# The first stage's stores, issued over three chunks instead of four and ahead of the x loads

## The chip, the cores and the metric

One core of a Trainium2 chip runs the kernel. The metric is the device time of one launch in microseconds (us), the median of several runs; smaller is better. Beside the times there is one execution taken by the hardware profiler, which gives start and length of every instruction on five engines: TensorE (PE; its weight loads are PEld), VectorE (DVE), ScalarE (ACT), GpSimd (POOL) and SyncE (SP). In this kernel SP and POOL also issue nearly all the DMAs: each puts them into a queue of its own, in the order of its program, and both queues are worked off by the same 16 DMA engines.

## The reference

Two layers run on x of shape (16, 192, 64, 64) in float32: 16 images, 192 channels, 64 by 64 pixels. Cut to what matters:

```python
h = layernorm_over_channels(x)                    # per pixel
pg = einsum('bchw,oc->bohw', h, in_proj_w) + b    # 192 -> 384 channels
projected, gate = split(pg, 2, axis=1)
projected = depthwise3x3(projected, dw_k)
scanned = four_directional_scans(projected)       # along rows and columns, both ways
local = depthwise3x3(projected, le_k)
mixed = (scanned + local) * sigmoid(gate)
x = x + conv1x1(gelu(batchnorm(mixed)), out_proj)
x = x + mlp(layernorm_over_channels(x))           # 192 -> 768 -> 192
# second layer: a depthwise masked 3x3 whose taps come from the mean of each image
```

The change touches only the part that computes `pg`, the normalised and projected x.

## The kernel before

The kernel has three stages. The first computes `pg` for all images and writes it to DRAM in an order that suits the second. The second takes groups of 8 channels at a time through the depthwise convolutions, the scans and the gate, and writes `mixed`. The third does the output projection, the MLP and the second layer.

The order of instructions on every engine is the order in which the program writes them: a `manual_schedule` covers PE, DVE, ACT, SP and POOL. A DMA instruction waits on its issuing engine until its buffers may be used, and what is written behind it on that engine waits too.

**The first stage** (lines 275 to 640) works on 64 chunks, `n` from 0 to 63. A chunk holds 4 groups of 128 pixels in each of two images. Four chunks (`per`) make a block; `blk, part = divmod(n, per)` gives the block and which quarter of it the chunk is. In one pass of the loop over n (L614):

- `load_a(n + 3)` (L499 to L507) loads the x of the chunk three ahead, in six DMAs of 128 KB (L505): three on SP for the first image, three on POOL for the second. Each moves runs of 512 bytes. The tile `xa` has four buffers, so that this load waits until PE has finished with chunk n - 1.
- `store_first` (L562 to L566) and `store(blk - 1, d, ...)` (L577 to L581) write the results of the block before. `PARTS` (L47) cuts the 24 groups of channels into five parts, d = 0 to 4, with 1, 7, 7, 5 and 3 groups; the very first group is kept on the chip by `store_first`. A store of one part is four DMAs, two on SP and two on POOL, of 64 KB per group: 64, 448, 448, 320 and 192 KB each.
- `turn(n + 1)` (L512) transposes the next chunk on PE (24 short matmuls, L518), from which DVE takes mean and variance over channels.
- `project(n, ...)` (L534) does the 48 matmuls of the chunk (L547) into PSUM, 12 for each group of pixels. DVE (L552, first image) and ACT (L553, second image) scale each group by its standard deviation and write it into the staging buffer of the block. There are two PSUM tiles per image, so PE can be two groups ahead of DVE and ACT.
- Work for later (weights, tables of decays, the matrices `dm` and `lm` of the second stage) is hung on given chunks by `beside(n, ...)` and run at the end of the chunk (L633).

**The staging buffer** is one of two: even blocks use `stg`, which exists once, odd blocks use `mid` (L538 to L541). The first write of block b therefore waits until all stores of block b - 2 have landed. Those stores are issued while block b - 1 is computed.

In the loop before the change, the loads and stores stand in this order:

```python
            if n + 3 < n_ac:
                load_a(n + 3)
            blk, part = divmod(n, per)
            if blk:
                if part == 0:
                    store_first(blk - 1)
                    store(blk - 1, 0, (nc.gpsimd, nc.sync))
                store(blk - 1, part + 1, (nc.gpsimd, nc.sync))
```

The names used further on: L44 is line 44, but "the load of pass 45" is `load_a(48)`, issued in pass n = 45 of the loop, and "S2" is `store(blk - 1, 2, ...)`.

Of the kernel before, what the change touches and what calls it, by code (L numbers as in the profile page):

```python
# [55 lines left out]
def conv_block_kernel(ctx: ExitStack, tc: tile.TileContext, x, prm, w_in, w_out, w_fc1, b_fc1, w_fc2, w1, bn1, w2, out):  # L56
    nc = tc.nc
# [217 lines left out]
    with ExitStack() as stage:  # L275
# [216 lines left out]
        n_ac = n_pairs * NCH  # L492
        per = BR // AR
# [5 lines left out]
        def load_a(n):  # L499
            blk, part = divmod(n, per)  # L500
            p, u = divmod(blk, 2)
            xa = xp.tile([128, 3, CH], F32, tag="xa", name="xa")
            for i, q in enumerate(HALF):
                for t in range(3):
                    (nc.sync, nc.gpsimd)[i].dma_start(  # L505
                        xa[q, t].rearrange("p (g n) -> p g n", n=128), xr[2 * p + i, u, :, t, part * AR:(part + 1) * AR])
            ast[n]["xa"] = xa  # L507
# [4 lines left out]
        def turn(n):  # L512

            xt = [psa.tile([128, 4, AR, 64], F32, tag=f"xt{i}", name=f"ps_xt{i}") for i in range(2)]
            for t in range(3):
                for g in range(AR):
                    for i, q in enumerate(HALF):
                        nc.tensor.transpose(xt[i][:, t, g], pixels(n, t, g)[q], ident[q, q])  # L518
            ast[n].update(xt=xt, st6=sp.tile([128, AR, 2, 6], F32, tag="st6", name="st6"),
                          mv=sp.tile([128, AR, 2, 2], F32, tag="mva", name="mva"))  # L520
# [7 lines left out]
        def deviation(n):  # L528
            rs = sp.tile([128, AR, 2], F32, tag="rsa", name="rsa")
            nc.scalar.activation(rs, ast[n]["mv"][:, :, :, 1], AF.Sqrt, bias=eps6)  # L530
            nc.vector.reciprocal(rs, rs)
            ast[n]["rs"] = rs

        def project(n, groups, beside_it):  # L534

            blk, part = divmod(n, per)
            if blk not in stag:
                if blk % 2:  # L538
                    both_i = mid.rearrange("p (i o j) -> p i o j", i=2, j=BR)
                else:  # L540
                    both_i = stg.tile([128, 2, 2 * C, BR], F32, tag="stg", name="stg")  # L541
                stag[blk] = [both_i[:, i] for i in range(2)]
            for g in groups:
                ps = [psa.tile([128, CH], F32, tag=f"pj{i}", name=f"ps_pj{i}", bufs=2)[:, 0:2 * C] for i in range(2)]
                for t in range(3):
                    for i, q in enumerate(HALF):
                        nc.tensor.matmul(ps[i], pixels(n, t, g)[q], wi[q, t].rearrange("p g k c -> p (g k c)"),  # L547
                                         start=(t == 0), stop=(t == 2))
                for v in beside_it(g) if n + 1 < n_ac else ():
                    variance(n + 1, v)  # L550
                j, rs = part * AR + g, ast[n]["rs"]
                nc.vector.tensor_scalar_mul(stag[blk][0][:, :, j], ps[0], rs[:, g, 0:1])  # L552
                nc.scalar.activation(stag[blk][1][:, :, j], ps[1], AF.Copy, scale=rs[:, g, 1:2])  # L553

        def each(blk):
            p, u = divmod(blk, 2)
            for i in range(2):
                ih, i8 = divmod(2 * p + i, n_half)
                for par, q in enumerate(HALF):
                    yield i, par, q, i8, 2 * u + par, HALF[ih]  # L560

        def store_first(blk):  # L562

            for i, par, q, i8, b, qh in each(blk):
                (nc.gpsimd, nc.sync)[par].dma_start(pg_even[qh, i8 * NB + b].rearrange("p k c j -> p (k c j)"),
                                                    stag[blk][i][q, 0:2 * GC].rearrange("p o j -> p (o j)"))  # L566
# [10 lines left out]
        def store(blk, d, queues):  # L577
            lo_, hi_ = PARTS[d]
            for i, par, q, i8, b, qh in each(blk):
                queues[par].dma_start(pg_d[d][i8, b, qh],  # L580
                                      stag[blk][i][q, lo_ * 2 * GC:hi_ * 2 * GC].rearrange("p o j -> p (o j)"))  # L581
# [30 lines left out]
        deviation(0)  # L612

        for n in range(n_ac):  # L614
            if n + 3 < n_ac:
                load_a(n + 3)
            blk, part = divmod(n, per)
            if blk:
                if part == 0:
                    store_first(blk - 1)  # L620
                    store(blk - 1, 0, (nc.gpsimd, nc.sync))
                store(blk - 1, part + 1, (nc.gpsimd, nc.sync))
                if part == per - 1:
                    stag.pop(blk - 1)

            h = AR // 2 if n == 0 else 0
            project(n, range(h), lambda g: ())
            if n + 1 < n_ac:
                turn(n + 1)
            project(n, range(h, AR), lambda g: (g,) if h == 0 else (2 * (g - h), 2 * (g - h) + 1))  # L630
            if n + 1 < n_ac:
                deviation(n + 1)
            for f, args in side.pop(n, ()):  # L633
                f(*args)
# [828 lines left out]
```

## Time and profile before

| | |
|---|---|
| median of three runs | 3542.76 us (3542.14 to 3543.65) |
| profiled execution, its own time | 3541.4 us |
| its span, first to last instruction | 3539.6 us |
| PE busy in the span | 3512.9 us (99%) |
| DVE, ACT, POOL busy | 2741.6, 1839.7, 1171.1 us |
| first stage | from 0 to about 581 us of the span |
| DMA in the first 600 us | 157.11 MB, mean 262 GB/s |

Times in the lines of the profile are in us from the start of the span. In a timeline, "x3" says that three like instructions stand side by side, and the two numbers ahead are the start of the first and the length of the whole run. In a list of waits, the name ahead of the arrow waited for the name behind it: total, number of times, longest. The chain of work that ended last is followed back from the end of the kernel; a stretch on it, if shortened, would have let the kernel end sooner. In a table of stretches, each engine has its busy time and its number of instructions; PEclk is the TensorE clock that was granted, as a share of full speed, and DMA is the mean busy share of the 16 DMA engines. Busy time of PE counts its matmuls with modelled ends.

### The profile page before, as it was taken

The numbers are of one execution on the slowest core, as the hardware profiler recorded it, in microseconds if no ns is written. First come the engines' busy times: TensorE is split into PE (matmuls) and PEld (weight loads), VectorE is DVE, ScalarE is ACT, GpSimd is POOL, SyncE is SP. The second block draws the span as 40 slices with busy tenths as digits, with TensorE's granted clock in tenths as the row PEclk, the third lists the DMA queues.
The fourth block names the chain that finished last, engine by engine and source line by source line (L and its number), as shares of the span: only waits on it lengthen the run. The fifth ranks groups of instructions, "written<-read, shape, count | busy, mean of one in ns | idle before, by whom it ended". The sixth has DMA issues, their size and how long they took to land.

```text
span 3539.6 us, 78530 instructions
## 1 busy us (share of the span) xinstructions
PE 3512.9 (99%) x33144; PEld 1919.0 (54%) x33144; DVE 2741.6 (77%) x4666; ACT 1839.7 (52%) x2086; POOL 1171.1 (33%) x1302
## 2 busy tenths in 40 slices
PE   9999999999999999999999999999999999999998
PEld 7666966566666754444444444444444444444444
DVE  7888777999999975557777777777677777767766
ACT  4444445888888844344444445454444444453543
POOL 3545432111111134333333334343333333343433
PEclk9999999999999999999999999999999999999999
DMA  6999999999999941112222223222222222232213
GB/s 178 269 271 276 272 272 310 288 289 285 277 285 286 248 119 34 40 55 61 70 68 74 66 65 82 59 75 63 79 61 70 68 74 65 66 83 58 75 34 90
DMA packets 288745, 492.00 MB, mean 139 GB/s; under 512 B 24752, under 2 KB 182824, under 8 KB 288392
## 3 DMA queue, kind: packets, MB, share of 16 engines
q1 hardware_dynamic: 246548, 341.57, 35.6%
q0 software_dynamic: 40912, 144.37, 14.2%
q8 instruction: 261, 4.28, 0.5%
q10 hardware_dynamic: 932, 1.03, 0.1%
q14 instruction: 92, 0.75, 0.1%
HBM read 284.95 MB, written 197.92 MB: 136 GB/s over the span
## 4 chain that ended last, share of the span: by engine, by line
PE 98%; DMA 1%; DVE 1%; issue 0%; ACT 0%; POOL 0%; SPq 0%; ACTq 0%; DVEq 0%
PE ps_f L1046 28%; PE ps_f L901 19%; PE ps_pj L547 14%; PE ps_l L718 12%; PE ps_d L674 7%; PE ps_s L901 7%; PE ps_o L956 5%; PE ps_o L949 2%; PE ps_xt L518 1%; PE ps_m L985 1%; PE ps_v L985 1%; DMA xa<-in_x_dram 0%; DVE ol L65 0%; PE ps_i L1259 0%; DVE o L65 0%
## 5 line engine op out<-in xcount | busy, mean ns | idle before, releaser
L1046 PE MATMUL ps_f<-h,wf 64*64 64x512 f32 x9216 | 1014.9, 590 | 0.0
L1048 ACT ACTIVATE gl<-ps_f,bf 128x1024 f32<-128x1024 f32 x384 | 428.2, 1115 | 1077.0 <-PE ps_f L1046 1076.7
L1046 PEld LDWEIGHTS ps_f<-h,wf 64*64 64x64 f32 x9216 | 346.2, 133 | 599.0 <-issue 574.9
L901 PE MATMUL ps_f<-gl,place 128*64 128x256 f32 (+1 forms) x3072 | 528.3, 486 | 1.1 <-ACT rs L1028 1.1
L547 PE MATMUL ps_pj<-wi,xa 64*128 64x384 f32 x3072 | 516.9, 487 | 7.1 <-DVE stg L552 6.8
L547 PEld LDWEIGHTS ps_pj<-wi,xa 64*128 64x128 f32 x3072 | 337.0, 188 | 151.6 <-DVE stg L552 9.3
L1081 POOL TENSOR_TENSOR gl<-gl 128x512 f32<-128x512 f32 x192 | 308.7, 1634 | 159.4 <-PE ps_f L901 159.4
L901 PEld LDWEIGHTS ps_f<-gl,place 128*64 128x64 f32 x3072 | 220.4, 137 | 222.4 <-issue 147.4
L1071 POOL COPY turn<-o 128x1 f32<-128x1 f32 x84 | 16.6, 197 | 820.9 <-DVE o L65 820.9
L1077 POOL TENSOR_TENSOR t<-gl 128x512 f32<-128x512 f32 x192 | 246.3, 1283 | 90.8 <-ACT gl L1048 46.4
L1079 POOL TENSOR_TENSOR t<-gl,t 128x512 f32<-128x512 f32 x192 | 247.5, 1289 | 43.8 <-ACT gl L1048 30.5
L65 DVE SCALAR_TENSOR_TENSOR o<-ximg,taps,o 128x1024 f32<-128x1024 f32 x180 | 231.7, 1288 | 4.9
L709 DVE TENSOR_TENSOR_SCAN v<-tab,q 128x1024 f32<-128x1024 f32 x96 | 218.3, 2274 | 5.6 <-ACT q L689 5.6
L711 DVE TENSOR_TENSOR_SCAN v<-tab,q 128x1024 f32<-128x1024 f32 x96 | 217.5, 2266 | 0.0
L505 POOL DMA_DIRECT2D xa<-in_x_dram x192 | 120.7, 635 | 274.4 <-PE ps_pj L547 238.7
L697 ACT ACTIVATE tab<-mask,dec_b 128x1024 f32<-128x1024 f32 x192 | 210.2, 1150 | 0.0
L1104 DVE SCALAR_TENSOR_TENSOR ximg<-ps_f,pt,ximg 128x256 f32<-128x256 f32 (+1 forms) x176 | 96.7, 549 | 145.6 <-PE ps_f L901 145.6
L553 ACT ACTIVATE stg<-ps_pj,rsa 128x384 f32<-128x384 f32 x128 | 119.5, 938 | 162.3 <-PE ps_pj L547 142.9
L553 ACT ACTIVATE mid<-ps_pj,rsa 128x384 f32<-128x384 f32 x128 | 119.2, 933 | 153.7 <-PE ps_pj L547 143.0
L962 DVE SCALAR_TENSOR_TENSOR ximg<-ps_o,pt,low 128x256 f32<-128x256 f32 x264 | 113.0, 479 | 93.8 <-PE ps_o L956 90.0
L956 PE MATMUL ps_o<-low,wo 128*64 128x256 f32 x1536 | 180.8, 384 | 0.0
L525 DVE BATCH_NORM_STATS2 st<-ps_xt 128x6 f32<-128x192 f32 x512 | 171.5, 335 | 4.6 <-PE ps_xt L518 4.0
(273 smaller groups left out, 5672.5 us busy)
## 6 DMA issues: line engine op xcount, KB each, us to landing
low<-in_x_dram SPq DMA_DIRECT2D x128, 384.0 KB
out_dram<-o SPq DMA_DIRECT2D x172, 256.0 KB
mid<-pg_d SPq DMA_DIRECT2D x8, 4096.0 KB
low<-mixed_d SPq DMA_DIRECT2D x116, 256.0 KB
low<-pg_d SPq DMA_DIRECT2D x7, 4096.0 KB
pg_o<-pg_d SPq DMA_DIRECT2D x7, 4096.0 KB
xa<-in_x_dram POOLq DMA_DIRECT2D x192, 128.0 KB, 5.1
xa<-in_x_dram SPq DMA_DIRECT2D x192, 128.0 KB
```

Of the source, the lines that this page charges most:

```text
L65: nc.vector.scalar_tensor_tensor(o, in0, scalar, in1, ALU.mult, ALU.add, **kw)
L547: nc.tensor.matmul(ps[i], pixels(n, t, g)[q], wi[q, t].rearrange("p g k c -> p (g k c)"), start=(t == 0), stop=(t == 2))
L553: nc.scalar.activation(stag[blk][1][:, :, j], ps[1], AF.Copy, scale=rs[:, g, 1:2])
L674: nc.tensor.matmul(dst(ps[o, ih]), mats[g % 2]["dm"][q, di + 1, :, ch], src(s["pg"][q, :, 0, ch]), start=(di == 0), stop=stop)
L718: nc.tensor.matmul(dst(bst[k]["ps"][o, i]), lm_of(g)[q, m, :, c], src(q, ih), start=start, stop=stop)
L901: nc.tensor.matmul(ps[q], w(i), rhs(i), start=start, stop=stop, **kw)
L956: nc.tensor.matmul(ps[wh][q].rearrange("p (r w) -> p r w", w=32), wo[:, 64 * t:64 * t + 64], cols(rows(s["mx"][:, i]))[:, :, wh], start=fi ...
L1046: nc.tensor.matmul(pf[o, i], wf1[q, t, m0:m0 + 64], s["h"][q, t], start=(t == 0), stop=(t == 2))
L1048: nc.scalar.activation(gl, pf, AF.Gelu, bias=bf1[:, m:m + 1])
L1077: sub(t1[:, m], b12(m), b11(m))
L1079: sub(t2[:, m], b22(m), t1[:, m])
L1081: sub(b12(m), b22(m), b12(m))
```

## The change

In the first quarter of a block nothing moves. In the second, S2 is issued ahead of the loads of x rather than behind them. In the third, S3 and S4 are issued ahead of the loads; before, S3 was issued behind them, and S4 behind those of the fourth quarter. In the fourth quarter only the loads are left.

```diff
         for n in range(n_ac):
-            if n + 3 < n_ac:
+            blk, part = divmod(n, per)
+            if part == 0 and n + 3 < n_ac:
                 load_a(n + 3)
-            blk, part = divmod(n, per)
             if blk:
                 if part == 0:
                     store_first(blk - 1)
-                    store(blk - 1, 0, (nc.gpsimd, nc.sync))
-                store(blk - 1, part + 1, (nc.gpsimd, nc.sync))
+                for d in ((0, 1), (2,), (3, 4), ())[part]:
+                    store(blk - 1, d, (nc.gpsimd, nc.sync))
                 if part == per - 1:
                     stag.pop(blk - 1)
+            if part and n + 3 < n_ac:
+                load_a(n + 3)
```

Nothing else differs: the same instructions with the same sizes are issued, and on PE, DVE and ACT the order is the same. `stag.pop` only forgets a name while the program is built.

## The prediction

> **What bounds the kernel now.** I read the page first.
>
> ```profile
> PE 3512.9 (99%) x33144; PEld 1919.0 (54%) x33144; DVE 2741.6 (77%) x4666; ACT 1839.7 (52%) x2086; POOL 1171.1 (33%) x1302
> ```
>
> PE is busy for 99% of the span, so a reordering of DMAs can win only where PE stands still in the first stage, and lose only by making it stand still. From the chain, taken in order of time, I read when each chunk's projection starts. The undisturbed pace is (429.82 - 344.46) / 10 = 8.536 us a chunk: 7.79 of projection, 0.74 of transposes. Two places with the same cause stand out, the first chunks of blocks 8 and 12 (n = 32, 48). The larger, in the chain between 425 and 460 us:
>
> ```profile
> 429.82 7.81 PE ps_pj L547 x47
> ...
> 441.87 4.73 DMA pg_d<-mid
> 446.60 0.01 issue
> 446.61 0.93 DVE stg L552
> 447.54 0.04 issue
> 447.58 5.83 PE ps_pj L547 x24
> 453.41 0.74 PE ps_xt L518 x24
> 454.15 5.85 PE ps_pj L547 x35
> ```
>
> From chunk 47 to chunk 49 it takes 454.15 - 429.82 = 24.33 us instead of 17.07, a loss of 7.26. DVE and ACT may not write `stg` until the stores of block 10 are out of it; the chain names `mid`, but `mid` is not what DVE writes here, so I take the name as an inference and look at SP's own timeline, from 405 us:
>
> ```profile
> 421.75 3.24 SPq L505 DMA_DIRECT2D xa<-in_x_dram  x3
> 425.03 2.54 SPq L580 DMA_DIRECT2D pg_d<-stg  x2
> 427.75 4.50 SPq L505 DMA_DIRECT2D xa<-in_x_dram  x3
> 432.30 2.17 SPq L580 DMA_DIRECT2D pg_d<-stg  x2
> 434.51 1.84 SPq L218 DMA_DIRECT2D dm<-dv_d  x1
> 436.53 2.27 SPq L505 DMA_DIRECT2D xa<-in_x_dram  x3
> 438.84 1.25 SPq L580 DMA_DIRECT2D pg_d<-stg  x2
> ```
>
> These are the loads of pass 45, S2, the loads of pass 46, S3, a matrix for the second stage, the loads of pass 47 and S4. S4 leaves only from 438.84 on, when PE is already in pass 48 (since 437.6): SP is most of a chunk late, and the store lands near 446.6. The small parameter loads just ahead (415.57 to 421.58) had held SP. The granted clock adds to it:
>
> ```profile
> 442.00:447.00 5.00, 0.28 (x2) 0.00 (x0) 0.40 (x1) 0.41 (x1) 0.92 (x2) 1.00 1.07 364
> ...
> 449.00:450.00 1.00, 1.00 (x6) 0.69 (x4) 0.93 (x5) 0.00 (x0) 0.00 (x0) 0.50 0.72 185
> ```
>
> PE is idle for 5.30 us (its wait for DVE) and then runs at 0.50 of its clock until about 451: 24 matmuls take 5.83 us instead of 3.9. So 5.30 + 1.93 = 7.2 of the 7.26. At n = 32 (chain: 290.84 to 309.72, 18.88 for two chunks) the loss is 1.81, with 1.52 idle and the clock at 1.00.
>
> [...] POOL stood 238.7 us in 49 waits of L505 for PE, with later stores behind it. [...] Of the first 600 us the DMA view gives SP's queue 73204 packets for 80.47 MB (1.10 KB each), POOL's 20766 for 75.42 MB (3.63 KB each)[...]. [...]
>
> **The change, part by part.** It issues the same 128 KB loads and the same stores. It does more than move S4 one pass up. `load_a` waits for PE to leave chunk n - 1, and that wait no longer stands ahead of S2, nor of S3 and S4. So S2 follows S1 at once in the first quarter, and S3 and S4 follow the second quarter's loads. Bytes by quarter, with a chunk's loads as 0.79 MB and a group as 0.26: before 3.1, 2.6, 2.1, 1.6; after 5.0, 2.9, 0.8, 0.8. At the 276 to 298 GB/s seen with full DMA engines, a chunk of 8.54 us passes some 2.4. A queue now builds up in the first half of a block and is drained in the second.
>
> *Gain, stores.* In block 11 I replay SP's rows in the new order, each with its own length: S2 421.75 to 424.3, loads of pass 45 to 427.5, S3 to 429.7, S4 to 431.0, loads of pass 46 to 434.2 (its 4.50 us contain waiting for PE; I leave 3.2). S4 leaves at 431.0 instead of 440.1. With the 6.5 us that it took before (440.09 to 446.6) it lands at 437.5; DVE wants the buffer after 439.8. The wait goes, with its half-speed clock: 7.26. At n = 32 S4 ends at 299.8 and the write comes at 303.85; some 5 us earlier (the fourth quarter's loads, 5.25, no longer stand ahead of it) removes 1.81. Together 9.07; both ends are sure within about 1 us, if nothing else holds the buffer.
>
> *Cost, SP's loads of x.* The loads of the second quarter move behind S2, those of the third behind S3 and S4. What counts is how much time is left between the end of their issue on SP and the transposes that need them, two chunks on. Before, from SP's timeline and the chain: pass 45, 425.0 to 428.96, 4.0 left; pass 46, 432.25 to 437.6, 5.4; pass 41, 6.7; pass 42, 7.8; the rest 8 to 15. PE waited for none, so one such load landed within 4.0 us of its issue. Taking off the issue time of the stores now ahead leaves: pass 45, 4.0 - 2.5 = 1.5; pass 46, 437.6 - 434.2 = 3.4, more if PE has lost time at pass 45's; pass 30, 298.5 - 287.1 - 4.95 - 2.24 = 4.2; pass 42, 4.9; pass 41, 5.4; the other second and third quarters 5.7 and more. The landing time is not shown for SP; on POOL a load takes 2.9 to 11.3 us, median 5.1. Lower bound 2.9: cost 1.4, at pass 45's loads alone. At 4.0: 2.5. At 5: pass 45 3.5, pass 30 0.8, pass 42 0.1, together 4.4. I take about 4.6: 3.1 and 0.4, together 3.5. Such a wait has no cover: the transposes stand ahead of the projection on PE, and DVE's statistics and the whole chunk follow. [...]
>
> *POOL's issues.* Four more stores at 0.53 to 0.55 us each are 1.1 to 2.2 us ahead of POOL's loads, hidden in its waits of 3.5 to 5.6 us for PE. POOL's ninth DMA in flight waits for the first (2.21 us at 442 us), so the denser order will show more such waits. Its loads have 17.1 us from pass to need; the slowest now needs about 11 plus the wait of pass 30. I charge nothing; without the cover it is about 1 us a block, 14 in all.
>
> *The end of the stage.* In block 15 no loads are left from pass 61 on; S4 moves ahead of the two loads of `wf1` (L70, L71), which are wanted at 594.2 and issued by 573. Nothing.
>
> Sum: -7.26 - 1.81 + 3.5 = -5.6 us. Against the profiled execution 3541.4 - 5.6 = 3535.8; the median of the runs is 1.4 above it, so 3542.76 - 5.6 = **3537.2**.
>
> **The rivals.**
> *All of the gain.* SP's loads land in time (below 3 us from issue, or S2 runs faster when it stands right behind the small loads). For it: SP idles between quarters in most blocks. Against it: pass 45 has 1.5 us left. -9.07 + 1.4 or less: 3533.7 to 3535.
> *SP's loads of x late in every block* (the one on the other side). Place: transposes of chunks 48, 33, 45 first, then all second and third quarters. Price by block at a landing time of 7.5 us: 0.9, 1.7, 0.4, 3.3, 1.8, 0.7, 2.6, 6.0 plus 1.9 of half clock, 1.5, 1.8, together 22.6; net +13.5, so 3556. It decides from 5.9 us of landing time on, where the loads cost the 9.1 gained. For it: POOL's median of 5.1 and the deeper queue ahead of the loads. Against it: the 4.0 bound, though that queue held small loads.
> *The wait stays.* DVE's wait was named after `mid`; if a DMA of the current block holds `stg`[...], S4's earlier issue saves little: 3541 to 3544. Against it: S4's times fit.
> That the change doesn't do what it says I exclude: the built order has the stores where the diff puts them, on SP and POOL alike.
>
> **How the numbers follow.** Chances: forecast 0.45 (3535.7 to 3540.5), all of the gain 0.23, the wait stays 0.14, loads late 0.18. About 0.2% (7.1 us) is what a measurement can tell from no change. Faster by more: all of the gain, and a little of the forecast, 0.26. Slower by more: most of the late case, 0.16. Within: 0.58. Range 3533 to 3549: it holds the first three cases and the mild part of the fourth, and leaves out about 0.17.
>
> **What would show it.** Right: no wait of DVE or ACT at L552 and L553 for a DMA at n = 32 and 48, no 0.50 clock near 450; S4 issued by SP about 9 us before pass 48; PE waits at L518 for `xa`, of 1 to 4 us at chunk 48. Wrong: PE waits for `xa` in most blocks (my landing time is too short), or the wait at n = 48 is still there (another holder of `stg`). The second and third stages should keep their lengths, 3539.6 - 581 us.

## The result, and the profile after

The changed kernel takes 3584.93 us in the median of four runs (3583.45 to 3593.89), the kernel before in the same series 3542.45 (3539.88 to 3543.65): a ratio of 1.0129, 95% interval 1.0117 to 1.0141, or 42.5 us slower. The forecast was 3537.2 with a range up to 3549. What happened is the rival "SP's loads of x late in every block", and at three times the size that it was given. One run of an experiment below (POOL alone ahead) took 3910.57 us at a granted clock of 0.887, the others of that kernel 0.995 to 0.997, and is in no number given.

The profiled execution has a span of 3584.0 us. The first matmul of the second stage's convolution starts at 628.23 us of it, before the change at 583.21: 45.0 us are lost in the first stage, and from there on the two kernels agree within 1 to 2 us. The line of engines on the page of the changed kernel:

```profile
PE 3529.0 (98%) x33144; PEld 1844.9 (51%) x33144; DVE 2745.4 (77%) x4666; ACT 1840.9 (51%) x2086; POOL 1169.0 (33%) x1302
```

PE does the same 33144 matmuls. It is idle for 3584.0 - 3529.0 = 55.0 us, before for 26.7, and its busy time has grown by 16.1 us. So the loss has two parts, standing still and running slower. The list of waits from 30 to 640 us says for what (who waited, for whom: total, times, longest):

```profile
PE ps_xt L518 <- DMA xa<-in_x_dram: 34.1, 17, 4.7
...
DVE stg L552 <- DMA xa<-in_x_dram: 2.4, 4, 0.6
```

Before, the first line did not exist. Now PE stands ahead of the transposes for a load of x 17 times, at 12 different chunks, 34.1 us in all. Asked who waited for the loads that SP issued, the same trace answers with all 17:

```profile
PE ps_xt L518: 34.1, 17
```

No wait of PE in this stretch ended with a load that POOL issued. The longest waits for `stg` of the kernel before were these:

```profile
ACT stg L553 <- DMA pg_d<-mid: 7.9, 1, 7.9
DVE stg L552 <- DMA pg_d<-mid: 6.8, 1, 6.8
```

They are gone: the two places of the forecast, n = 32 and 48, no longer lose their 1.8 and 7.4 us (by the starts of the transposes). With the 9.2 us that this gains, the late loads of x cost 45.0 + 9.2 = 54 us, of which 34 are waits.

One block shows how. The chain of work from 360 to 400 us, in block 9 (start, length, what):

```profile
363.75 0.74 PE ps_xt L518 x21
364.49 5.45 PE ps_pj L547 x29
369.94 15.41 DMA xa<-in_x_dram
385.36 0.14 issue
385.49 1.63 PE ps_xt L518 x24
387.13 9.17 PE ps_pj L547 x48
396.30 0.74 PE ps_xt L518 x24
```

A load of x that SP began to issue at 369.94 has landed at 385.36. PE stood still from 380.83 to 385.49, 4.66 us. After that the 24 transposes take 1.63 us instead of 0.74 and the projection 9.17 instead of 7.79: another 2.27 us. SP's own timeline for the same block (start, length, instruction):

```profile
355.29 2.79 SPq L505 DMA_DIRECT2D xa<-in_x_dram  x3
358.18 1.19 SPq L565 DMA_DIRECT2D low<-stg  x2
359.42 10.35 SPq L580 DMA_DIRECT2D pg_d<-stg  x6
369.94 6.93 SPq L505 DMA_DIRECT2D xa<-in_x_dram  x3
376.92 7.76 SPq L580 DMA_DIRECT2D pg_d<-stg  x4
```

The third line holds S0, S1 and S2; the loads behind it are those of pass 37. The six stores keep SP for 10.35 us and the three loads for another 6.93. Their issue ends at 376.87, and the last lands 8.5 us after that. Before the change the same block had the loads between S1 and S2, with shorter times for all:

```profile
338.79 5.41 SPq L580 DMA_DIRECT2D pg_d<-stg  x4
344.38 6.19 SPq L505 DMA_DIRECT2D xa<-in_x_dram  x3
350.61 2.67 SPq L580 DMA_DIRECT2D pg_d<-stg  x2
```

So the loads are late twice over: SP takes longer to issue what stands ahead of them, and they then take longer to land (8.5 us, where PE waited for no load of pass 45 before, which had 4.0). The two DMA queues over 359 to 372 us (packets, MB, share of the 16 engines' time; the software queue is POOL's, the hardware queue SP's):

```profile
q0 software_dynamic: 484, 2.18, 73.3%
q1 hardware_dynamic: 926, 1.03, 28.1%
```

The engines are full (the two shares add to 101.4%), and POOL's queue has nearly three quarters of their time. SP's moves 1.03 MB in 13 us, 79 GB/s, while S0 to S2 and three loads put 1.97 + 0.39 MB into it. So in this block the burst fills the engines, and of the two queues it is SP's that falls behind. The table of stretches gives the clock (us, busy time of PE, PEld, DVE, ACT and POOL, then PEclk, DMA share, GB/s):

```profile
381.00:384.00 3.00, 0.00 (x0) 0.00 (x0) 1.00 (x2) 0.93 (x2) 1.83 (x3) 0.83 0.95 275
384.00:387.00 3.00, 1.51 (x26) 1.54 (x26) 0.00 (x0) 0.00 (x0) 0.00 (x0) 0.50 1.03 375
387.00:389.00 2.00, 2.00 (x11) 1.16 (x10) 0.98 (x4) 0.00 (x0) 0.00 (x0) 0.50 0.91 300
389.00:391.00 2.00, 2.00 (x14) 1.23 (x12) 0.48 (x1) 0.44 (x1) 0.00 (x0) 0.80 0.71 165
```

PE's clock falls to 0.50 during the wait, at 382.96, and stays there until 389.79. This comes back in block after block: the first chunk of every block from n = 16 to 60 except 28 waits (n = 16, 20, 24 and so on), and by the starts of the transposes it and the chunk after it lose between 2 and 7 us together in most blocks, by the waits and by transposes and projection at the lower clock. The loads that are late are those of the second quarter, the ones behind S2; of the third quarter's, PE waited for one, 0.6 us at chunk 29.

### The profile page after: what moved, and what is told of

It reads as the page before. It is cut to its first block, busy times and chain, and to the rows that moved or that the text cites. A ratio compares the mean times of both kernels' runs of the same rounds, so it can differ in the third digit from the quotient of the medians.

```text
span 3584.0 us, 78532 instructions
## 1 busy us (share of the span) xinstructions
PE 3529.0 (98%) x33144; PEld 1844.9 (51%) x33144; DVE 2745.4 (77%) x4666; ACT 1840.9 (51%) x2086; POOL 1169.0 (33%) x1302
## 3 DMA queue, kind: packets, MB, share of 16 engines
q10 hardware_dynamic: 932, 1.03, 0.1%
## 4 chain that ended last, share of the span: by engine, by line
PE 94%; DMA 5%; DVE 1%; SPq 1%; issue 0%; ACT 0%; ACTq 0%; DVEq 0%
PE ps_f L1048 28%; PE ps_f L903 18%; PE ps_l L720 12%; PE ps_pj L547 11%; PE ps_d L676 7%; PE ps_s L903 7%; PE ps_o L958 5%; DMA xa<-in_x_dram 4%; PE ps_o L951 2%; PE ps_xt L518 1%; PE ps_m L987 1%; PE ps_v L987 1%; SPq L505 0%; DVE o L65 0%; PE ps_i L1261 0%
## 5 line engine op out<-in xcount | busy, mean ns | idle before, releaser
L547 PE MATMUL ps_pj<-wi,xa 64*128 64x384 f32 x3072 | 525.4, 496 | 0.1
L547 PEld LDWEIGHTS ps_pj<-wi,xa 64*128 64x128 f32 x3072 | 310.6, 192 | 179.6 <-issue 12.4
L505 POOL DMA_DIRECT2D xa<-in_x_dram x192 | 119.2, 626 | 275.0 <-PE ps_pj L547 200.6
```

## The experiments

Every kernel below computes all of the reference. Edits are shown against the changed kernel, where nothing else is said; the kernel before that each ratio refers to ran on the same chip. "PE's wait for x" is its wait at the transposes for a load of x between 30 and 640 us. "Own queue" means that a load is late because of what stands ahead of it in the queue of its own issuing engine; "shared" that the 16 engines are full, whatever queue the bytes are in.

**The packing alone: stores over three quarters, all of them behind the loads.**

```diff
-            if part == 0 and n + 3 < n_ac:
+            if n + 3 < n_ac:
                 load_a(n + 3)
...
-            if part and n + 3 < n_ac:
-                load_a(n + 3)
```

> The stores of a block in three chunks as in the change (S0 and S1, S2, S3 and S4, none), but every store behind its pass's loads of x, so that the wait of the loads for PE stands ahead of the stores again. Theory A, the order (stores ahead of the loads make the loads of the second quarter land after the transposes need them): no wait of PE for xa after the first chunks, and the waits for the staging buffer at chunks 32 and 48 gone or much shorter, since S4 leaves some 5 to 9 us earlier: 3533 to 3538 us. Theory B, the three chunks (the stores packed into three quarters overfill the DMA engines, wherever they stand): waits for xa remain in most blocks, 3560 us or more.

Measured: 3537.19 us against 3542.77, ratio 0.9982 (0.9975 to 0.9988), 5.6 us faster. The second stage starts at 579.54 instead of 583.21. The waits for `stg` at 32 and 48 are gone here too. Its chain of work keeps two loads of x, in block 11:

```profile
428.18 4.04 DMA xa<-in_x_dram
...
441.91 7.67 DMA xa<-in_x_dram
```

and its list of waits has what is left of PE's:

```profile
PE ps_xt L518 <- DMA xa<-in_x_dram: 4.0, 3, 2.3
```

So the gain is real, and it needs only the denser stores. The loss is not in the density: it needs stores ahead of loads.

**Which of the two moves: only S2 ahead of the loads, then only S3 and S4.**

```diff
 # only S2
-            if part == 0 and n + 3 < n_ac:
+            if part != 1 and n + 3 < n_ac:
...
-                for d in ((0, 1), (2,), (3, 4), ())[part]:
+                for d in ((0, 1), (2,), (3,), (4,))[part]:
...
-            if part and n + 3 < n_ac:
+            if part == 1 and n + 3 < n_ac:
```

```diff
 # only S3 and S4
-            if part == 0 and n + 3 < n_ac:
+            if part != 2 and n + 3 < n_ac:
...
-            if part and n + 3 < n_ac:
+            if part == 2 and n + 3 < n_ac:
```

> Only S2 ahead of its pass's loads of x; S3 and S4 in their old places, behind the loads of the third and the fourth quarter. If S2 is what delays the loads of the second quarter: PE waits for xa once a block as after the change, for 2 to 5 us, and the time is 3570 to 3590 us. If it takes S3 and S4 as well (POOL's S3 and S4, issued at once behind the second quarter's loads, overtake SP's loads in the engines): the waits are mostly gone, 3540 to 3552 us. The long wait for the staging buffer at chunk 48 stays or shrinks, as PE is later.

> Only S3 and S4 ahead of the loads of the third quarter; S2 in its old place behind the loads of the second. If S2 is the cause: no regular wait for xa, S4 early, 3533 to 3541 us. If S3 and S4, brought forward, delay the second quarter's loads: waits once a block remain, 3560 us or more. If they delay the third quarter's own loads: waits once a block, but one chunk later in the block (the transposes of its first chunk).

Measured: only S2 3575.13 us, 1.0096 (1.0079 to 1.0114), 32 us slower; only S3 and S4 3564.62 us, 1.0060 (1.0045 to 1.0075), 22 us slower. PE's wait for x with S2 alone ahead:

```profile
PE ps_xt L518 <- DMA xa<-in_x_dram: 26.0, 19, 3.7
```

and with S3 and S4 alone ahead:

```profile
PE ps_xt L518 <- DMA xa<-in_x_dram: 18.6, 15, 2.8
```

In the first the late loads are those of the second quarter, as in the changed kernel. In the second they are mostly those of the third quarter, wanted at chunks 13, 29, 33 and so on; the forecast that S2 is the cause alone fell. In both places the stores put ahead make the loads behind them late: 26.0 and 18.6 us of waits, against 4.0 with every store behind the loads. The two effects add to 54, not to 42. A reading that fits, but that no run isolates: where the second quarter's loads are late, PE is late too, and the third quarter's loads have that time as a present.

**More time for the same order: a fifth buffer for x, loads four chunks ahead.** A matrix tile of the second stage that is free until then serves as the fifth buffer.

```diff
-            xa = xp.tile([128, 3, CH], F32, tag="xa", name="xa")
+            if n % 5 == 4:
+                xa = mats[1]["dm"].rearrange("p k m c -> p k (m c)")
+            else:
+                xa = xp.tile([128, 3, CH], F32, tag="xa", name="xa")
...
-                load_a(n + 3)
+                load_a(n + 4)
```

> The change, with five buffers for x (the fifth in the place of a matrix of the second stage that is loaded only at pass 60) and the loads issued four chunks ahead, so that each has three chunks' time (25.6 us) instead of two (17.1) to land. If the loads are late by their place in the queue alone: no waits for xa, no waits for the staging buffer, 3532 to 3538 us. If the stage has become bound by what the DMA engines can move: the waits stay, only later, 3560 us or more.

Measured: 3543.58 us, 1.0001 (0.9992 to 1.0009). Of its list of waits:

```profile
ACT stg L556 <- DMA pg_d<-mid: 8.4, 1, 8.4
...
DVE stg L555 <- DMA pg_d<-mid: 5.7, 1, 5.7
...
PE ps_xt L521 <- DMA xa<-in_x_dram: 1.2, 1, 1.2
```

One chunk more of time takes 34.1 us of PE's waits down to 1.2, so the loss is lateness, and not that the DMA engines can't keep up in the mean. It did not give the 9 us on top that were expected, because the wait for `stg` at n = 48 is there again. SP's timeline has S3 and S4 of block 10 in one row:

```profile
436.10 4.05 SPq L583 DMA_DIRECT2D pg_d<-stg  x4
```

They end at 440.15, where S4 alone ended before the change (440.09), though the order has them a quarter earlier: SP itself runs that much late. ACT writes at 445.67. By the starts of the transposes chunks 49 to 51 lose 1.6, 6.3 and 1.4 us, 9.3 in all, where 1.8 and 7.4 were lost before: nothing is won, and +0.8 was measured.

**Place in the queue, or the moment of departure: one of three loads ahead of the stores.** The first load of each image waits for PE ahead of the stores, so that these leave as late as before; the other two stand behind them. The second argument of `load_a` says which of the three to issue.

```diff
-            if part == 0 and n + 3 < n_ac:
-                load_a(n + 3)
+            if n + 3 < n_ac:
+                load_a(n + 3, (0, 1, 2) if part == 0 else (0,))
...
-                load_a(n + 3)
+                load_a(n + 3, (1, 2))
```

> The change, with one of the three loads of each half (t = 0) issued ahead of the stores in the second and third quarter, the other two behind them. The wait of the loads for PE then stands ahead of S2, S3 and S4 again, so the stores leave at their old time; but two thirds of the loads still stand behind them. If the early departure of the stores is what fills the engines before the loads come: the waits for xa shrink to a few, 3538 to 3552 us. If the place in the queue alone is what matters: two thirds of the loads are still late and PE waits once a block, 3565 us or more.

Measured: 3591.16 us against 3539.93, 1.0135 (1.0116 to 1.0155). PE's wait for x is as in the changed kernel:

```profile
PE ps_xt L520 <- DMA xa<-in_x_dram: 35.7, 22, 4.5
```

and SP's timeline in block 9 shows the order:

```profile
363.37 1.63 SPq L507 DMA_DIRECT2D xa<-in_x_dram  x1
365.05 3.46 SPq L582 DMA_DIRECT2D pg_d<-stg  x2
368.55 7.38 SPq L507 DMA_DIRECT2D xa<-in_x_dram  x3
```

S2 leaves only when PE has released the buffer, and nothing is won. So that the stores leave early, while SP would have stood waiting for PE, is not the cause; that the loads are behind them is.

**Which queue: all of S2 on SP, then all of S2 on POOL.**

```diff
-                    store(blk - 1, d, (nc.gpsimd, nc.sync))
+                    store(blk - 1, d, (nc.sync if d == 2 else nc.gpsimd, nc.sync))     # on SP
+                    store(blk - 1, d, (nc.gpsimd, nc.gpsimd if d == 2 else nc.sync))   # on POOL
```

> The change, with all four DMAs of S2 on SP, none on POOL. If a load is late by what stands ahead of it in its own queue: SP's loads of the second quarter stand behind 0.9 MB more, and PE waits longer in each block, by 2 us or more; 3605 us or more. If it is late by the sum of what both queues hold[...]: no change, 3575 to 3595 us.

> The change, with all four DMAs of S2 on POOL, none on SP. By the own queue: SP's loads of the second quarter stand behind S0 and S1 only and land in time, POOL's come later but have more room; 3540 to 3565 us. By the sum of both queues[...]: SP's loads land as late as before this edit, 3575 to 3595 us.

Measured: on SP 3599.65 us, 1.0164 (1.0149 to 1.0179); on POOL 3552.38 us, 1.0036 (1.0024 to 1.0049). The bytes are the same, and the place ahead of the loads too; only the queue differs, and the two lie 47 us apart. With S2 on SP, block 9 has eight stores in one row, and PE waits 11 us more than in the changed kernel. SP's timeline:

```profile
366.15 14.31 SPq L580 DMA_DIRECT2D pg_d<-stg  x8
380.64 7.00 SPq L505 DMA_DIRECT2D xa<-in_x_dram  x3
```

PE's wait for x with S2 on SP:

```profile
PE ps_xt L518 <- DMA xa<-in_x_dram: 45.2, 17, 6.0
```

With S2 on POOL the list of waits reads:

```profile
POOL pg_d L580 <- DMA pg_d<-stg: 47.0, 25, 3.2
...
POOL pg_d L580 <- DMA pg_d<-mid: 27.4, 17, 3.2
...
PE ps_xt L518 <- DMA xa<-in_x_dram: 12.1, 16, 1.7
```

Of these 12.1 us, 11.2 are for loads of SP, which still stand behind S0 and S1 or S3 and S4, and 0.9 for loads of POOL, though POOL has all of S2 ahead of them. So which queue S2 is in decides most of the loss, as "own queue" says. Why POOL bears it is less clear: POOL now stands before its stores, 74 us in 42 waits for stores of its own to land, so its stores also leave later and more spread out, and no run separates this from the queue. S2 on SP lies between the two marks: the queue's length counts, but less than forecast.

**One queue at a time: the stores ahead of the loads on SP alone, then on POOL alone.**

```diff
-                load_a(n + 3)                                        # head
+                load_a(n + 3, (0, 1) if part == 0 else (1,))         # SP's loads behind
...
-                load_a(n + 3)                                        # tail
+                load_a(n + 3, (0,))
```

The second argument of `load_a` says which halves to load: 0 on SP, 1 on POOL. For POOL alone the halves are exchanged.

> The change on SP alone: there S2, S3 and S4 stand ahead of the loads; on POOL the loads stand ahead of the stores of their pass. If the order on SP's own queue is the whole cause: nearly the time of the change, 3575 to 3590 us. If both queues have a part: clearly less, 3550 to 3570 us.

> The change on POOL alone: there S2, S3 and S4 stand ahead of the loads; on SP the loads stand ahead of the stores of their pass (as in the run with all stores behind). If only the order on SP's own queue makes loads late: no regular wait for xa, and 3 to 7 us below the kernel before. If POOL's early stores delay SP's loads in the shared engines: waits once a block, 3555 us or more.

Measured, against 3541.96: SP alone 3565.55 us, 1.0055 (1.0037 to 1.0073), 23.6 slower; POOL alone 3544.88 us, 1.0008 (0.9999 to 1.0017), 2.9 slower and by its interval not told apart from the kernel before. PE's wait for x with SP alone, then with POOL alone:

```profile
PE ps_xt L521 <- DMA xa<-in_x_dram: 20.5, 15, 3.9
```

```profile
PE ps_xt L521 <- DMA xa<-in_x_dram: 10.6, 7, 4.7
```

With POOL alone the loads of SP stand ahead of the stores again. Asked who waited for the loads that SP issued, its trace gives all of the 10.6 us:

```profile
PE ps_xt L521: 10.6, 7
```

With every store behind the loads it was 4.0. So POOL's early stores make the loads of SP late, across the two queues; POOL's own loads ended no wait of PE. All three kernels contain the packing too, which alone gave 0.9982. Against that, SP's order alone costs 0.0073 (26 us), POOL's alone 0.0026 (9 us) and both together 0.0147 (52 us), more than the sum: SP's own stores are the larger part, and POOL's add to them. In the changed kernel POOL's loads of x land 7.4 us after issue in the median, before the change 5.1.

**Was SP late at block 11 because of the small parameter loads?** Those of passes 44 and 50 are moved to 51 and 56, once in the kernel before and once in the kernel with all stores behind the loads.

```diff
-        for k in (0, 3, 4):
-            beside(40 + k, load_weights, k)
+        for k, n in ((0, 40), (3, 43), (4, 51)):
+            beside(n, load_weights, k)
...
-        beside(50, squeeze_scale)
+        beside(56, squeeze_scale)
```

> The kernel before, with one edit: the small parameter loads of pass 44 (four DMAs on SP, 6 us of its time) moved to pass 51, and the preparation that reads one of them from pass 50 to 56. If these loads are what made S4 of block 10 late on SP: S4 leaves some 6 us earlier, the wait at chunk 48 and the half clock after it are gone or nearly so, and the time is 5 to 7 us below the kernel before of the same chip; the 1.8 us at chunk 32 stay. If something else holds the staging buffer: the wait stays and so does the time.

> The stores in three chunks, each behind its pass's loads, and the small parameter loads of pass 44 (four DMAs on SP, 6 us of its time) moved to pass 51, with the preparation that reads one of them moved from pass 50 to 56. The three chunks alone took away the waits for the staging buffer, but left PE waiting for the loads of passes 45 and 46 (4.0 us and 7.7 us of chain near 432 and 450). If SP's parameter loads are the cause of these too: no wait of PE between 100 us and the end of the stage, 3532 to 3535 us. If not: as the three chunks alone, 3536 to 3539 us.

Measured: in the kernel before 3536.78 us against 3541.96, 0.9986 (0.9978 to 0.9993); on top of the stores behind the loads 3534.48 against 3539.93, 0.9982 (0.9975 to 0.9989), the same ratio as without, and PE still waits for x three times, 2.9 us in all (4.0 without). The first has the time that was expected, but hardly for the reason given. SP's timeline and one line of DVE's, in the kernel before with the parameters moved:

```profile
438.51 1.25 SPq L580 DMA_DIRECT2D pg_d<-stg  x2
```

```profile
304.74 0.94 DVE L552 TENSOR_SCALAR stg<-ps_pj,rsa 128x384 f32<-128x384 f32 x1 [4.58 <-DMA pg_d<-mid]
```

S4 leaves at 438.51, before the edit at 438.84. PE comes to pass 48, which wants the buffer, 2.15 us later than before (439.43 instead of 437.28), so against PE's progress S4 leaves 2.5 us earlier, of the 6 expected. The loss at n = 48 has shrunk from 7.4 to 1.15 us, while that at n = 32, where nothing was moved, has grown from 1.8 to 5.1, and n = 56 loses 2.0: together 8.25 where it was 9.2, so most of the 5.2 us gained isn't explained by these places. The parameter loads are then at most a part of what held S4; what else did is open. Each trace is one execution, and the times of the kernel before spread from 3537.03 to 3546.90 us in 27 runs, so how much one place loses may also change from run to run. The kernels with every store behind the loads and packed into three quarters have the lowest ratio, 0.9982; it is not told apart from the 0.9986 of the kernel before with the parameters moved, and moving the parameters on top adds nothing that can be measured.

## Why the prediction was wrong, step by step

**What bounds the kernel: right.** PE was full, and the order of DMAs could only make or remove standstill of PE in the first stage. All 45 us lie there.

**Gain, stores: right in the sum, in part by luck.** The waits for `stg` at n = 32 and 48 went, 9.2 us for the 9.07 worked out, and the kernel with the same packing and no store ahead of a load keeps 5.6 of it. But the replay's times are not what removed the wait everywhere. In that kernel SP ends S4 of block 10 at 439.20, hardly earlier than before (440.09), and the wait at n = 48 is gone because PE, which waited 4.0 us for x, comes to pass 48 at 440.36 instead of 437.28, and because S4 had landed by 443.33 at the latest (446.6 before). In the changed kernel PE is late as well, by its waits for x. The reason given for SP's lateness, the small parameter loads, is supported at most in part.

**Cost, SP's loads of x: the step that failed.** Worked out as 3.5 us; late loads of SP cost 54. The mechanism, loads late behind the stores, was named; three terms of the sum were mis-sized, and with them the number of blocks that wait. The sign of being wrong that the prediction gave for this, PE waiting for `xa` in most blocks, is what came.
- *The time from the end of issue to landing*: taken as 4.6 us, measured 8.5 in block 9. The bound of 4.0 came from one load, that of pass 45, which stood behind small transfers; it could not bound loads behind two megabytes of stores. The prediction named this doubt and gave it too little weight.
- *Issue time on SP*: the replay gave each DMA the length that it had before. In block 9 that makes 8.1 us for the six stores and 6.2 for the loads, and 7.4 us are left to the transposes. They took 10.35 and 6.93, and 3.8 were left; with 8.5 us to land, PE waits 4.7. The time on SP did not stay the same: SP's issues of stores from `stg` took 0.73 us in the median before the change, 1.52 with the packing alone and 1.90 in the changed kernel, the same stores each time. Both errors are of one kind: the state of the queue was taken from an order in which it was shorter.
- *The clock*: half clock was charged to one wait for x in the late case (1.9 us), to none in the forecast. That such waits would leave the clock alone was the author's estimate; the kernel before showed only two places, 5.30 us of idle time with the clock at 0.50 after it and 1.52 with the clock at 1.00. About 54 - 34 = 20 us of the loss are not waits. PE worked for 32.1 us of the first stage at a clock of 0.50; at 1.00 the same work would take half of that, so 16 us, an estimate from these two numbers, are lost there; the other 4 are not traced. The 4.66 us of idle time in block 9 are part of it, and shorter ones too (see the last section).

**POOL's issues: charged nothing, right for POOL's own loads, wrong for what its stores do to SP's.** In block 9 POOL's loads of pass 37 landed 10.1 to 11.7 us after issue, and in time: no wait of PE ended with a load of POOL. What was left out is the other queue. With POOL's stores alone ahead PE waits 10.6 us for loads of SP, with none ahead 4.0.

**The end of the stage, the later stages: right.** Nothing there moved by more than 2 us.

**The rivals.** "SP's loads of x late in every block" named the place (all second and third quarters; it was nearly all second ones), the sign and the condition: it decides from 5.9 us of landing time on, and the time was 8.5. Its price, 22.6 us at 7.5 us, took over the replay's issue times and only 1.9 us of half clock, and so came to less than half. "The wait stays" fell in the changed kernel; in the one with five buffers the wait at n = 48 is back, with S3 and S4 issued no earlier than S4 was before; whether SP's lateness is all of its cause was not tested. "All of the gain" fell.

**The range** ended at 3549, below even the middle of the late case, since that had 0.18 of the chance. The profile spoke for more: before the change the first 600 us already moved 262 GB/s with the 16 engines busy for 0.91 of the time, and the change puts 5.0 and 2.9 MB into two quarters that pass 2.4 each. The prediction wrote this down and then priced one load at a time.

## What to carry to other kernels

With the DMA engines as full as here (0.91 of the first 600 us before the change), loads of x put behind a burst of stores in the same queue landed late: 8.5 us after the end of their issue in block 9, and PE waited 4.66 us. So keep loads that the busiest engine will need ahead of stores that nobody waits for soon, and buy earlier stores by packing them behind the loads. Price such a move by bytes, queue by queue (what stands ahead, divided by what that queue moves when both are full), and not by the issue times and the fastest landing of the old order. In block 9 this estimate comes near: 1.97 + 0.39 MB at 79 GB/s are 30 us, and from the start of S0 on SP to the landing of the last load it took 26. A wait of PE can cost more than itself: the 4.66 us in block 9 were followed by a clock of 0.50 and another 2.27 us, so look at the clock just after a wait.

## What the runs showed of the hardware

*The two queues were not alike.* The queues interfere here, as POOL's stores that delay SP's loads show (10.6 us of waits, 4.0 without). And the choice of queue decided much: the same S2 in the same place gave 3599.65 us all on SP and 3552.38 all on POOL. In the stretch at 359 to 372 us SP's queue got 28% of the engines' time and POOL's 73%, with 926 packets of 1.1 KB to 484 of 4.5 KB. A delay shows at different places: in the changed kernel POOL's issues of loads and stores (L505, L580) take 0.52 to 0.68 us each, and POOL stands ahead of its stores (74 us in 42 waits with S2 on POOL), while SP's issues themselves grow longer (those of stores from `stg` 0.73 us in the median before, 1.90 in the changed kernel). Why the engines' time is divided so no run shows.

*The clock fell after idle times of 3.10 and 3.12 us, and not after one of 3.62.* In the changed kernel PE is idle for 3.10 us up to 153.01, and for another 0.45 up to 154.46, and the clock is 0.50 from 154.27 to 157.68. PE is idle for 3.62 us up to 425.53, and the clock stays at 1.00:

```profile
149.50:154.26 4.76, 1.41 (x20) 0.77 (x16) 1.34 (x4) 1.03 (x2) 1.84 (x3) 1.00 0.98 313
154.28:157.67 3.39, 3.21 (x18) 2.01 (x20) 0.98 (x4) 0.00 (x0) 0.00 (x0) 0.50 0.65 191
157.69:161.10 3.41, 3.41 (x24) 2.06 (x22) 2.38 (x6) 1.60 (x2) 1.16 (x2) 1.00 0.57 165
420.52:423.92 3.40, 1.39 (x10) 0.51 (x6) 2.33 (x7) 1.52 (x3) 1.68 (x3) 1.00 0.91 258
423.93:427.33 3.40, 1.80 (x30) 1.56 (x32) 0.62 (x3) 0.00 (x0) 0.14 (x1) 1.00 1.01 323
```

In the kernel before with the parameters moved, 3.12 us of idle time were enough:

```profile
307.00:309.00 2.00, 2.00 (x8) 1.02 (x6) 1.08 (x5) 0.00 (x0) 0.00 (x0) 0.50 0.83 211
```

In the changed kernel two gaps of 1.30 and 1.25 us with eight transposes between them, at 303 to 308 us, also ended in a clock of 0.50. At 345.41 it fell after gaps of 0.85 and 0.58 us with eight transposes between them. In the kernel before, the gap of 5.30 us began at 442.28, and the clock fell only at 447.60, at its end, and was back at 1.00 at 451.02. So in these traces the length of one gap does not decide alone. Between 20 us and the end of the first stage the changed kernel has the clock at 0.50 eight times: from 154.27, 195.23, 307.87, 345.41 and 464.88 on for 3.41 us each, from 382.96, 502.43 and 543.39 on for 6.83 us each. What decides when the clock falls no run shows.
